# Routing of seven image pairs placed inside the attention-only steps, with the first expert weights loaded early

## The chip, the cores and the metric

The program runs on one core of a Trainium2 chip. A core has a matrix engine (TensorE, PE), three engines for vectors and scalars (VectorE or DVE, ScalarE or ACT, GpSimd or POOL), an engine that mostly issues transfers (SyncE, SP) and 16 DMA engines. Each engine takes its own instructions in program order, and the engines wait for one another through semaphores. SP and ACT issue DMAs on queues of their own; GpSimd issues DMAs through software. The metric is the time of one execution on the device, in microseconds. Before the change three runs took 10483.3 to 10494.0 us, with a median of 10486.95 us.

## What is computed

The input is 16 images of 128 channels and 64 x 64 pixels, which make 16 batches of 4096 tokens. Layer 0 adds a state-space block: a group norm, projections, a short convolution and a scan over time with 16 states for each of 256 channels. Layer 1 adds a causal attention with 8 heads and then a mixture of 64 experts. In the mixture each expert chooses its 8 best tokens of each batch, over the whole of the batch:

```python
t = t + _L1_attn_ref(_ln_t(t), ...)
t = t + _L1_ffn_ref(_ln_t(t), gate_w, gate_b, weight1, weight2)
...
logits = jnp.einsum('bsd,ed->bse', x, gate_w) + gate_b
probs = jax.nn.softmax(logits, axis=1)              # over the tokens
vals, idx = jax.lax.top_k(probs.transpose(0, 2, 1), K)
...
pooled = jnp.einsum('bked,bke->bed', gathered, topv)
h = gelu(pooled @ weight1 + bias1)                  # per expert
out = h @ weight2 + bias2
weighted = jnp.einsum('beo,bke->bkeo', out, topv)
outputs = zeros.at[flat_idx].add(weighted)          # back to the tokens
```

So the routing of a batch needs the logits of all its 4096 tokens, and the experts need the routing of all the batches. "Routing" below is everything from the tokens after attention to the pooled vectors: the layer norm's statistics, the logits, the softmax over tokens, the eight largest, the gate weights (zero outside the chosen tokens) and their product with the normed tokens.

## The kernel before

The work is cut into 128 blocks, 8 of 512 tokens in each batch. The main loop runs over steps `k`. In step `k` the scan of block `k` is made, with the attention of block `m = k - 9` beside it. Each step has 16 rows, one for each state `n`. In a row VectorE makes the product `bx` and two halves of a scan `h`, GpSimd multiplies `h` by the broadcast row `bct` into `da`, and the table `STEP` (line 725) names the other operations of the row: those in its first part come ahead of the scan, those in the second between the scan's halves, those in the third after it. All are issued through `InOrder`, which keeps each engine's instructions in the order of the program.

Names of the table that matter here: `k0` to `k7` are the keys of eight heads, `s0` and `s1` the scores, `mx` and `less` the running maximum (VectorE), `w0` and `w1` the weights of the two halves of a block, `a..` the attention sums, `to0` and `to1` (`take_o`, line 703) the copy of half a block of output, tokens on partitions, into `ot`. In the next step `tu0`, `tu1` (`turn_o`, line 708) turn it to channels on partitions and `fin0`, `fin1` (`finish`, line 715) copy it and store it in `t2_d` from ScalarE's queue. `lnap` makes the normed block `xn`. `spread` loads small pieces of the scores through SP after they were stored in `pd`.

Short tiles (`ot`, `tx`, keys `kt` and others) come from the pool `tmp`, which has six buffers (line 226), taken in turn. The broadcast rows come through SP three rows ahead (`load_bc`, line 369), into five buffers; SP waits for GpSimd to release one. TensorE's results share a pool of three banks (`bank`).

The scans end with step 127. Steps 128 to 137 hold what is left of attention: step 128 finishes the last scanned block, and steps 129 to 136 have one whole attention block each. Step 137 has the second half of the last one.

Then the pools are closed, and the routing runs as a stage of its own (lines 858 to 1048), in 64 iterations. An iteration takes one 512-token block of two batches, a pair. It loads `t2_d` with channels on partitions (SP), turns it on TensorE, takes the statistics on VectorE and makes the normed tokens `xn` on ScalarE, eight activations. The logits come out with tokens on partitions (16 small matmuls), are scaled, and are turned back so that experts lie on partitions. After eight iterations `choose` (line 975) takes the exponential, the eight largest and the gate weights `g`, stored in `g_d`. Twelve iterations behind, `g` is turned and multiplied with the `xn` that were kept.

The experts follow (line 1071), in 16 groups of four. Each group loads 2 MB of weights through SP into four buffers, and its result is stored in `o_d`. The last stage (line 1107) multiplies the experts' results by `g` and adds them to the tokens.

Of the kernel before, what the change touches and what calls it, by code (L numbers as in the profile page):

```python
# [15 lines left out]
P = 128  # L16
# [23 lines left out]
def conv_attn_hybrid(ctx: ExitStack, tc: tile.TileContext, x, w_in, conv_w, conv_b, w_xproj, w_dt, b_dt,  # L40
# [26 lines left out]
    t2_d = dram.tile([NB, C, T], F32, name="t2_d")  # L67
    g_d = dram.tile([NB // 2, P, T], F32, name="g_d")
# [13 lines left out]
    with ExitStack() as st:  # L82
# [3 lines left out]
        yps = st.enter_context(tc.tile_pool(name="yps", bufs=1, space=PSUM))  # L86
        bps = st.enter_context(tc.tile_pool(name="bps", bufs=1, space=PSUM))
# [26 lines left out]
        wv = wp.tile([P, HD, P], F32, name="wv")  # L114

# [101 lines left out]

        xp = st.enter_context(tc.tile_pool(name="xp", bufs=1))
        xsp = st.enter_context(tc.tile_pool(name="xsp", bufs=2))
        xbp = st.enter_context(tc.tile_pool(name="xbp", bufs=2))  # L220
        mp = st.enter_context(tc.tile_pool(name="mp", bufs=2))
        m1 = st.enter_context(tc.tile_pool(name="m1", bufs=1))
        dap = st.enter_context(tc.tile_pool(name="dap", bufs=13))
        hp_ = st.enter_context(tc.tile_pool(name="hp", bufs=2))
        bcp = st.enter_context(tc.tile_pool(name="bcp", bufs=5))
# [481 lines left out]

        def turn_o(m, f):
            s = att[m]
            s["to"] = bank("to_ps")  # L710
            ot = s.pop("ot")
            for q in range(2):
                PE.transpose(s["to"][:, bass.ts(q, P)], ot[:, bass.ts(q, P)], ident)

        def finish(m, f):
# [5 lines left out]

        LAG = NBLK + 1
# [4 lines left out]
            ("k3 k4 skip k5 tu0 fin0", "", ""),  # L727
# [6 lines left out]
            ("ge4 xproj", "tu1 fin1 cen v0 y5", "bcs"),  # L734
# [44 lines left out]

        for k in range(NK + LAG + 1):  # L780
            b, i = divmod(k, NBLK)
            cur = k if k < NK else None
# [37 lines left out]
            for f in range(2):  # L820
                ops[f"tu{f}"] = (mp_, lambda m, f=f: turn_o(m, f))
                ops[f"fin{f}"] = (mp_, lambda m, f=f: finish(m, f))
# [18 lines left out]
            for n in range(N):  # L841
# [13 lines left out]
                do(n, 2)  # L855

# [3 lines left out]
    ff = ctx.enter_context(tc.tile_pool(name="ff", bufs=1))  # L860
    pooled = ff.tile([P, E, 32], F32, name="pooled")
    nc.gpsimd.memset(pooled, 0.0)
    with ExitStack() as st:
        PE, DVE, ACT, POOL, SP = (InOrder(tc, e) for e in (nc.tensor, nc.vector, nc.scalar, nc.gpsimd, nc.sync))
        NG = CB * 2
        LATE = 12
        AHEAD = 5
        xps = st.enter_context(tc.tile_pool(name="rxps", bufs=2, space=PSUM))
        lps = st.enter_context(tc.tile_pool(name="rlps", bufs=1, space=PSUM))
        sps = st.enter_context(tc.tile_pool(name="rsps", bufs=1, space=PSUM))  # L870
        acc = st.enter_context(tc.tile_pool(name="racc", bufs=1, space=PSUM))
        big = st.enter_context(tc.tile_pool(name="big", bufs=2))
        tsp = st.enter_context(tc.tile_pool(name="tsp", bufs=12))
        xnp = st.enter_context(tc.tile_pool(name="xnp", bufs=LATE + 3))
        rp_ = st.enter_context(tc.tile_pool(name="rp", bufs=2))

        def bank():
            return sps.tile([P, CB, P], F32, tag="s", name="s_ps")

        cmat = rp_.tile([P, P], F32, name="cmat2", bufs=1)  # L880
        DVE.tensor_tensor(cmat, ident, mean_w, ALU.subtract)
        gn = rp_.tile([E, C], F32, name="gn", bufs=1)
        SP.dma_start(gn, gate_w)
        gb = rp_.tile([P, 1], F32, name="gb", bufs=1)
        for j in range(2):
            SP.dma_start(gb[j * E : (j + 1) * E, :], gate_b.unsqueeze(1))
        gt_ps = bank()
        PE.transpose(gt_ps[:, 0, :E], gn, ident[:E, :E])
        gt = rp_.tile([P, E], F32, name="gt", bufs=1)
        DVE.tensor_copy(gt, gt_ps[:, 0, :E])  # L890
        gc_ps = bank()
        PE.matmul(gc_ps[:, 0, :E], cmat, gt, start=True, stop=True)
        gtc = rp_.tile([P, E], F32, name="gtc", bufs=1)
        DVE.tensor_copy(gtc, gc_ps[:, 0, :E])
        tc.keep_in_program_order(nc.scalar.preload_act_table_set(EXP_LN))

        NIT = NB // 2 * NBLK
        blk, pair = {}, {}

        def load_tokens(it):  # L900
            p, i = divmod(it, NBLK)
            w = blk[it] = {}
            w["t"] = [tsp.tile([P, L], F32, tag="t", name="t") for _ in range(2)]
            for j in range(2):
                SP.dma_start(w["t"][j], t2_d[2 * p + j, :, bass.ts(i, L)])

        def turn(it):
            w = blk[it]
            w["x"] = xps.tile([P, CB, 2, P], F32, tag="x", name="x_ps")
            for c in range(CB):  # L910
                for j in range(2):
                    PE.transpose(w["x"][:, c, j, :], w["t"][j][:, bass.ts(c, P)], ident)
# [9 lines left out]
        def stats(it):  # L922
# [3 lines left out]
            for g in range(NG):  # L926
                DVE.bn_stats(s6[:, g, :], w["x"][:, g // 2, g % 2, :])
# [220 lines left out]
```

## Time and profile before

| what | value |
|---|---|
| median of three runs | 10486.95 us |
| profiled execution, its own time | 10479.5 us |
| its span, first to last instruction | 10477.5 us |
| TensorE busy | 8614.8 us, 82% |
| VectorE busy | 9138.0 us, 87% |
| ScalarE busy | 7589.4 us, 72% |
| GpSimd busy | 7169.5 us, 68% |
| DMA traffic | 1783.37 MB, mean 170 GB/s |
| mean granted TensorE clock | 0.916 of full speed |

Busy shares are means over stages with different limits. The scans fill most of the span and keep VectorE at 0.9, so a share of the whole says little of the stages after them; those are read from windows of their own. In a group's row the busy time is the union of its instructions' intervals, while the mean is that of one instruction from start to end; where matmuls overlap, the busy time divided by the count is what one more of them costs.

### The profile page before, as it was taken

What the parts mean: (1) busy time and instruction counts of PE and PEld (TensorE: products, weight loads), DVE (VectorE), ACT (ScalarE), POOL (GpSimd) and SP (SyncE); (2) the same over time, 40 slices, a digit from 0 to 9 for tenths busy, and PEclk for the clock granted to TensorE, in tenths of its full rate; (3) what the DMA queues carried; (4) which work ended last, traced back from release to release, by engine and by line L of the source; (5) the groups of instructions that cost most, each with busy time, mean ns of one, the idle gap of its engine ahead of it and who ended that gap; (6) DMA issues with size and microseconds to landing.
All of it is one profiled execution on the core that took longest, in us unless ns stands there. A gap on an engine that the chain in (4) does not pass through costs nothing.

```text
span 10477.5 us, 183327 instructions
## 1 busy us (share of the span) xinstructions
PE 8614.8 (82%) x69084; PEld 5193.8 (50%) x69084; DVE 9138.0 (87%) x9089; ACT 7589.4 (72%) x14186; POOL 7169.5 (68%) x4476
## 2 busy tenths in 40 slices
PE   5578888888888888888888888888888888877775
PEld 3345554555555545554555554555555555544652
DVE  8999999999999999999999999999999999921743
ACT  5568777777777777777777777777787777755740
POOL 7887777777777777777777777777777777710000
PEclk7789999999999999999999999999999999999886
DMA  6676666666676666666666667666666666621358
GB/s 165 171 184 172 178 170 181 164 174 177 166 183 171 181 169 176 173 181 165 172 181 169 181 164 185 168 179 170 178 173 168 177 168 180 163 66 44 115 164 342
DMA packets 978008, 1783.37 MB, mean 170 GB/s; under 512 B 194953, under 2 KB 275489, under 8 KB 967905
## 3 DMA queue, kind: packets, MB, share of 16 engines
q1 hardware_dynamic: 724480, 1381.32, 45.4%
q0 software_dynamic: 82944, 302.03, 14.6%
q10 hardware_dynamic: 169696, 88.30, 3.0%
q8 instruction: 544, 8.91, 0.3%
q14 instruction: 344, 2.81, 0.1%
HBM read 1363.99 MB, written 138.94 MB: 143 GB/s over the span
## 4 chain that ended last, share of the span: by engine, by line
PE 26%; DVE 23%; ACT 20%; DMA 11%; issue 8%; POOL 4%; SPq 1%; ACTq 0%; DVEq 0%; POOLq 0%
DVE h L31 10%; DVE bx L31 8%; ACT da L31 6%; PE k_ps L31 5%; DMA da<-da 5%; PE ao_ps L31 5%; PE v_ps L31 4%; POOL da L31 4%; PE y_ps L31 4%; DMA bct<-bcs 3%; ACT L31 3%; DVE zl L31 2%; PE s_ps L31 1%; ACT xn L31 1%; DMA pd<-parts 1%
## 5 line engine op out<-in xcount | busy, mean ns | idle before, releaser
L31 POOL TENSOR_TENSOR da<-h,bct 128x1024 f32<-128x1024 f32 x2048 | 6334.3, 3098 | 1966.0 <-DVE h L31 766.2
L31 DVE TENSOR_TENSOR_SCAN h<-da,state,bx 128x512 f32<-128x512 f32 x3584 | 4399.7, 1266 | 187.6 <-DVE bx L31 1.9
L31 DVE TENSOR_TENSOR bx<-du,bct 128x1024 f32<-128x1024 f32 x2048 | 2892.8, 1412 | 272.3 <-DMA bct<-bcs 214.0
L31 ACT ACTIVATE da<-delta,a_neg 128x512 f32<-128x512 f32 x4096 | 2676.5, 718 | 73.1 <-DMA da<-da 47.1
L31 PE MATMUL y_ps<-ident,da 128*128 128x128 f32 x12288 | 1795.9, 299 | 632.0 <-POOL da L31 563.3
L31 PEld LDWEIGHTS y_ps<-ident,da 128*128 128x128 f32 x12288 | 1563.1, 155 | 1139.2 <-POOL da L31 624.5
L31 PE MATMUL k_ps<-xn,wk 128*128 128x512 f32 x2048 | 1087.4, 670 | 9.7 <-DVE xn L31 9.7
L31 PE MATMUL v_ps<-wv,xn 128*64 128x512 f32 x4096 | 1031.8, 612 | 75.9 <-ACT v L31 65.0
L31 PE MATMUL xs_ps<-xb,wc 128*128 128x512 f32 x2048 | 974.4, 608 | 1.8 <-issue 1.8
L31 ACT ACTIVATE v<-v_ps 128x512 f32<-128x512 f32 x1024 | 599.9, 596 | 369.7 <-PE v_ps L31 365.4
L31 ACT ACTIVATE kt<-k_ps 128x512 f32<-128x512 f32 x1024 | 609.3, 597 | 328.5 <-PE k_ps L31 317.8
L31 ACT ACT_TABLE_LOAD x633 | 812.1, 1283 | 21.1 <-ACT dbl L31 3.9
L31 PE MATMUL ao_ps<-v,wm 128*64 128x128 f32 x8192 | 608.5, 295 | 219.9 <-ACT wm L31 219.9
L31 PEld LDWEIGHTS ao_ps<-v,wm 128*64 128x64 f32 x8192 | 478.5, 146 | 336.2 <-ACT wm L31 282.7
L31 DVE TENSOR_TENSOR_SCAN h<-da,bx 128x512 f32<-128x512 f32 x512 | 598.1, 1207 | 27.1
L31 PEld LDWEIGHTS k_ps<-xn,wk 128*128 128x128 f32 x2048 | 415.2, 219 | 415.1 <-issue 322.8
L31 POOL COPY state<-h 128x2 f32<-128x2 f32 x1792 | 620.7, 346 | 0.0
L31 PEld LDWEIGHTS xs_ps<-xb,wc 128*128 128x128 f32 x2048 | 364.4, 193 | 470.2 <-issue 375.2
L31 ACT COPY yt<-y_ps 128x512 f32<-128x512 f32 x256 | 137.5, 589 | 624.2 <-PE y_ps L31 624.2
L31 PEld LDWEIGHTS v_ps<-wv,xn 128*64 128x64 f32 x4096 | 224.7, 135 | 674.7 <-ACT v L31 269.9
L31 POOL DMA_DIRECT2D da<-da x512 | 461.7, 902 | 99.3 <-POOL state L31 66.1
L31 PE MATMUL z_ps<-xb,wz 128*128 128x512 f32 x512 | 284.8, 639 | 118.5 <-ACT xc L31 100.3
(208 smaller groups left out, 10480.6 us busy)
## 6 DMA issues: line engine op xcount, KB each, us to landing
bct<-bcs SPq DMA_DIRECT2D x2048, 512.0 KB
da<-da POOLq DMA_DIRECT2D x512, 512.0 KB, 7.5
xs<-t_d SPq DMA_DIRECT2D x240, 256.0 KB
xs<-in_x_dram SPq DMA_DIRECT2D x128, 256.0 KB
t_d<-xt SPq DMA_DIRECT2D x64, 512.0 KB
t_d<-tx ACTq DMA_DIRECT2D x256, 128.0 KB
t<-t_d SPq DMA_DIRECT2D x128, 256.0 KB
tc<-t_d SPq DMA_DIRECT2D x16, 2048.0 KB
```

What stands on the lines that cost most here:

```text
L31: return lambda *args, **kw: self.tc.keep_in_program_order(f(*args, **kw))
```

## The change

Attention's output is stored a second time, with tokens on partitions, in a new array `t2t_d` (`store_tokens`, two SP stores of 128 KB for each block, `st0` and `st1` in the table). This is done in all steps with attention, those beside scans among them.

The scan's pools are put on the other side of the memory, so that they can be closed after step 128. In their place a class `routing` opens pools of its own: 4 of the 8 banks, and buffers for its tiles. From step 129 on, after each row, `route.row` is called; two rows make a slot. A slot treats up to one block of a pair in each of three phases, which follow one another through the steps:

- statistics: GpSimd loads token rows (`xa`), VectorE takes eight `bn_stats`. At the end of a step, `scales` makes the inverse deviations of a pair from these without `bn_aggr`. They are turned and stored in `rs_d`.
- logits: SP loads `t2_d` (`rt`) and the inverse deviations broadcast over the experts (`rb`); two matmuls with 512 columns give the logits with experts on partitions, and VectorE multiplies them into `lg`. The gate matrix is centred once, in the prologue.
- pooling: GpSimd loads the token rows again (`xd`). TensorE turns `g`, VectorE scales it by the inverse deviation, and TensorE multiplies it with the raw tokens. The mean is taken out at the end of a pair (`center_pooled`).

`choose` (row 15), `mark` (row 1) and `keep_chosen` (rows 2 and 3) of a pair come one and two steps later. `g` is no longer divided by the sum of exponentials; that division goes to `center_pooled` and to the last stage. Seven pairs are routed in this way. The last pair's statistics run there too, but for the last block. The rest of it is done after the loop, in `rest`, ahead of which SP issues the loads of the first four groups of expert weights. Weights have five buffers in place of four.

```diff
+        def store_tokens(m, f):
+            b, i = divmod(m, NBLK)
+            at = i * L + f * (L // 2)
+            SP.dma_start(t2t_d[b, at : at + L // 2, :].rearrange("(q p) c -> p q c", p=P),
+                         att[m]["ot"][:, : 2 * P].rearrange("p (q c) -> p q c", c=C))
...
+                self.t = pool("rtt", 4)
+                self.xa = pool("rxa", 3)
+                self.xd = pool("rxd", 2)
+                self.rb = pool("rrb", 2)
...
+            def load_stats(self, it):
+                p, i = divmod(it, NBLK)
+                x = self.w["a", it] = self.xa.tile([P, CB, 2, P], F32, tag="xa", name="xa")
+                for j in range(2):
+                    POOL.dma_start(x[:, :, j, :], t2t_d[2 * p + j, bass.ts(i, L), :].rearrange("(c p) d -> p c d", p=P))
...
+            def logits(self, it):
+                l = self.w["l", it] = self.lps.tile([P, L], F32, tag="l", name="l_ps")
+                t = self.w.pop(("t", it))
+                for j in range(2):
+                    PE.matmul(l[j * E : (j + 1) * E, :], gtc, t[j], start=True, stop=True)
...
+            def choose(self, p):
...
+                w["top"], w["den"] = top, self.sm.tile([P, 1], F32, tag="den", name="den")
+                ACT.activation(w["g"], w["lg"], AF.Exp, bias=neg, accum_out=w["den"])
+
+            def mark(self, p):
+                w = self.pair[p]
+                DVE.match_replace(out=w["lg"], in_to_replace=w.pop("top"), in_values=w["lg"], imm_value=NEG)
...
+                if half == 0:
+                    for it in at(D0 + 1, EARLY):
+                        self.pool_chosen(it)
+                    for it in at(B0, EARLY):
+                        self.logits(it)
+                    for it in at(D0, EARLY):
+                        self.turn_chosen(it)
...
+                    return
+                for it in at(D0, EARLY):
+                    self.scale_chosen(it)
+                for it in at(B0, EARLY):
+                    self.keep_logits(it)
+                for it in at(1, 8, 2) + [x for x in at(6 - 8, EARLY) if x >= 8]:
+                    self.stats(it)
...
+                for it in at(0, 8, 2) + [x for x in at(5 - 8, EARLY) if x >= 8]:
+                    self.load_stats(it)
...
+                for it in at(B0 - 1, EARLY):
+                    self.load_scales(it)
+                for it in at(B0 - 2, EARLY):
+                    self.load_logits(it)
+                for it in at(D0 - 1, EARLY):
+                    self.load_chosen(it)
+
+            def row(self, r):
+                step, n = divmod(r, N)
+                self.slot(r // 2, n % 2)
+                if step < NPR - 1:
+                    if n == 11:
+                        self.scales(step)
...
+                if n == 15 and 1 <= step <= NPR - 1:
+                    self.choose(step - 1)
+                if 2 <= step <= NPR:
+                    if n == 1:
+                        self.mark(step - 2)
+                    if n in (2, 3):
+                        self.keep_chosen(step - 2, n - 2)
...
+        B0, D0 = 8, 18
...
-            ("k3 k4 skip k5 tu0 fin0", "", ""),
+            ("k3 k4 skip k5 st0 tu0 fin0", "", ""),
...
-            ("ge4 xproj", "tu1 fin1 cen v0 y5", "bcs"),
+            ("ge4 xproj", "st1 tu1 fin1 cen v0 y5", "bcs"),
...
+                if route is not None:
+                    route.row((k - NK - 1) * N + n)
...
+    WAHEAD = 4
+    for e0 in range(0, WAHEAD * EG, EG):
+        load_weights(e0)
+    route.rest()
...
             nc.sync.dma_start(on, o_d[2 * pr : 2 * pr + 2].rearrange("b e o -> (b e) o"))
+            nc.vector.tensor_scalar(on, on, rden[:, pr : pr + 1], None, ALU.mult)
```

## The prediction

> **What bounds the kernel now.** I read the page first, for the slices of the span, then the busy times of four stretches, then the groups of instructions inside the routing stage, the waits of the attention-only steps, and last the order of time in one steady step and among the experts.
>
> The page's slices, each a fortieth of the span (262 us), in tenths:
>
> ```profile
> DVE  8999999999999999999999999999999999921743
> ...
> POOL 7887777777777777777777777777777777710000
> ...
> DMA  6676666666676666666666667666666666621358
> ```
>
> For 35 slices VectorE is at 0.9: the scans. Then VectorE and GpSimd fall to almost nothing, though the kernel runs for 1,250 us more. The windows split this tail (columns: us, then busy us and count of PE, PEld, DVE, ACT, POOL, then clock, DMA share, GB/s):
>
> ```profile
> 9436.00:9477.00 41.00, 33.02 (x344) 17.68 (x338) 2.11 (x7) 24.59 (x53) 0.00 (x0) 0.96 0.09 24
> ...
> 9750.00:9850.00 100.00, 79.47 (x704) 70.37 (x706) 79.05 (x295) 71.45 (x181) 0.00 (x0) 0.90 0.36 117
> ...
> 10175.00:10246.00 71.00, 52.78 (x500) 20.04 (x492) 8.16 (x17) 4.78 (x8) 0.00 (x0) 0.62 0.72 223
> 10246.00:10360.00 114.00, 67.75 (x124) 29.45 (x124) 39.34 (x61) 0.00 (x0) 0.00 (x0) 0.62 0.88 361
> ```
>
> The first is one attention-only step (period 41.9 us): TensorE and ScalarE hand work to each other, VectorE works 2.1 us, GpSimd not at all, DMA 0.09. The second is routing, where TensorE, VectorE and ScalarE are all busy; the third the experts, the fourth the last sum, which the transfers bound. The last scan starts at 9229.3, the last attention store is issued at 9641, the first weights' load at 10106.7 and the last sum's first load about 10246; I put the borders at 9231 (attention only), 9643 (routing), 10107 (experts) and 10246, so they last 412, 464, 139 and 231 us.
>
> Groups in the routing stage (busy us, mean ns, idle before):
>
> ```profile
> L31 ACT ACTIVATE xn<-x_ps,nm,rs 128x128 f32<-128x128 f32 x512 | 185.5, 474 | 0.0
> ...
> L31 DVE BATCH_NORM_STATS2 s<-x_ps 128x6 f32<-128x128 f32 x512 | 107.3, 285 | 10.8 <-PE x_ps L31 10.6
> ...
> L31 PE MATMUL pl<-xn,gT 128*64 128x128 f32 x1024 | 76.6, 297 | 0.0
> ...
> L31 DVE TENSOR_TENSOR ls<-l_ps,rs 128x512 f32<-128x512 f32 x64 | 43.9, 686 | 0.3 <-PE l_ps L31 0.3
> L31 PE MATMUL s_ps<-ident,g 128*128 128x128 f32 x256 | 43.0, 295 | 5.7 <-DVE g L31 3.2 <-ACT gT L31 1.7 <-ACT lg L31 0.8
> ...
> L31 DVE MAX8 top<-lg 128x8 f32<-128x1024 f32 x32 | 38.5, 1202 | 1.9 <-ACT lg L31 1.7 <-issue 0.3
> L31 DVE SCALAR_TENSOR_TENSOR g<-g,sden,rep 128x2048 f32<-128x2048 f32 x16 | 37.3, 2334 | 0.0
> ...
> L31 DVE MATCH_REPLACE8 rep<-top,lg 128x4096 f32<-128x4096 f32 x8 | 35.3, 4409 | 0.0
> ...
> L31 ACT ACTIVATE g<-lg,neg 128x4096 f32<-128x4096 f32 x8 | 30.1, 3757 | 0.0
> ```
>
> Back-to-back matmuls overlap, so I price TensorE by a group's busy time over its count, not by the mean. In the attention steps' groups the keys give the price of a 512-column matmul:
>
> ```profile
> L31 PE MATMUL k_ps<-xn,wk 128*128 128x512 f32 x128 | 58.9, 603 | 0.0
> ```
>
> that is 0.46 us. And in time order, in a steady step of the main loop, ScalarE's attention output, the key five places on, and GpSimd's product that frees the SP queue's next buffer:
>
> ```profile
> 5040.88 0.36 ACT L31 COPY ot<-ao_ps 128x256 f32<-128x256 f32 x1
> ...
> 5056.95 0.58 ACT L31 ACTIVATE kt<-k_ps 128x512 f32<-128x512 f32 x1
> ```
> ```profile
> 5037.54 2.36 POOL L31 TENSOR_TENSOR da<-h,bct 128x1024 f32<-128x1024 f32 x1 [0.30 <-DVE h L31]
> ```
>
> **The Trainium skill.** "DMA: Bandwidth & Descriptors", section "Anatomy of one DMA — SWDGE (gpsimd) path", gives a fixed cost of about 2 us per DMA from GpSimd and calls descriptor generation "small, variable". The trace has 902 ns on GpSimd per da<-da DMA and 7.5 us to its landing, under the main loop's traffic. The same page, section "Queues, rings and completion order", says that an engine consumes a queue's descriptors in ring order and takes turns between queues; so the early weights delay what SP issues after them, not GpSimd's loads. "Specifications" there asks for at least 512 B per piece; the token rows are just that. Half of the weight bytes before are also 512 B rows, and that stage reached 328 GB/s in one 8 us window.
>
> **The change, part by part.**
>
> *Main loop.* The engines' order is unchanged. Added are two SP stores of 128 KB per step, 119 steps with attention before the scans end. A store holds the buffer of ot until it has landed, and `tmp` has six: the sixth key, kt at 5056.95, takes that buffer. SP reaches st0 when GpSimd's product above is done (5039.9), waits for ot (5041.2), and should land by about 5045: 12 us to spare. Behind SP's wait stand the B/C loads, but the next one needs a GpSimd product that ends at 5048. st1 waits for ot at 5009.8, 1.5 us before its successor's buffer is free. As engine time, 256 KB at 310 GB/s is 0.8 us a step, 100 us in all if nothing covered it; VectorE's waits for bct come behind the small spread loads, 11 us after st1. I take 5 us; bounds 0 and 100. The gate's preparation moves to the prologue, about 1 us, left out.
>
> *Removed.* The 464 us stage. Gone outright are the transposes of x, 512 xn activations (185 us of ScalarE), the turning of logits and its copies. Removing the aggregation and not_equal spares VectorE too.
>
> *Moved.* One block per two rows, eight per step, in nine steps. Per block TensorE: pooling 76.6/64 = 1.20, turn of weights 43.0/64 = 0.67, two logits matmuls 0.92: 2.8 us, 22.3 per full step. VectorE: eight stats 2.28, scaling 0.69, logits 0.69, max 0.60: 4.25 us a block, 34 a step, with match_replace 4.4, two products 4.7, the last pair's block 2.3 and small ones 1.5 it is 47, and 49 with attention's 2.1. ScalarE: 24.6 + 4.0 (the exponential) + 0.6 = 29. Transfers: xa, xd and rt 4.2 MB each, rb and g_d 2.1 each, attention 1.2: 18 MB, at 310 GB/s 58 us. GpSimd: 32 DMAs. Its price is not shown for 512 pieces: at da's 0.9 us it is 29 us, in proportion to pieces (128 there) 3.6 us, 115 a step. I take 1.2 us, 38 a step, since the skill calls generation small; both ends go to the range.
>
> So TensorE needs 33 + 22.3 = 55 us a full step, transfers 58, VectorE 49. They are in-order and coupled. Of the 8.9 us that TensorE waits today I let blocks cover 5 to 6 (its waits for wm stand right behind a block) and keep 3. New: at row 15 `choose` puts 4 us on ScalarE, and behind it the table load and all keys; its bias waits for VectorE to finish block 15 (5 us). TensorE has three banks of keys and one block (5.5 us) before it stops; it loses about 5.4. VectorE's mark and products stand ahead of `mx` in rows 1 to 3, and xd is loaded only 1.5 blocks ahead: 4 us together. Sum 33 + 22.3 + 3 + 5.4 + 4 = 68 us. Steps that are not full: k=129 has no TensorE blocks (44), k=130 logits only (50), k=131 (62), then four of 68, k=136 without xa loads (65), k=137 has half an attention step, 25 us, and eight blocks (45). From 9273 that is 538: 9811.
>
> *Last pair, `rest`.* Drain of five blocks 12; SP's loads behind 8.4 MB of weights (27 us, begun in the middle of the last step) 5; eight logits, each load 0.75 MB reissued two ahead, 2.5 each: 20; choose, mark (which must wait for the exponential, as it writes lg in place) and two products 13.5; eight poolings over two xd buffers, each pair about 8.6 us (two DMAs of 1.2, landing 5, pooling 1.2) from the third on: 29; centre and turn 2. Sum 82: 9893.
>
> *Experts.* Five groups of weights can be there. Without missing weights a group takes TensorE and its hand-overs 7.2 to 7.4 us before (hs at 10164.09, 10171.53); 16 make 117, with the end 121, against 139. The other 11 groups are 23 MB, 75 us, hidden. *Last sum*: eight small scalings more; 231.
>
> Sum: 9893 + 121 + 231 + 5 = 10250 as span. The profiled execution took 10479.5, 2.0 more than its span, and 7.5 less than the median of the runs shown; I forecast 10255 us.
>
> **The rivals.**
>
> *GpSimd's issuing and the transfers bound the steps.* At 3 us per DMA a block takes 12 us, a full step 96. Four steps lose 112, the two beside them about 30, the last pooling 10: 10405 us. For it: four DMAs of 512 pieces per block, and DMA already at 58 us. Against it: GpSimd is otherwise empty.
>
> *The waits are all covered.* Blocks fill TensorE's waits and a full step takes 58, the transfers' time: 45 to 60 us less, 10200 us. For it: ScalarE at 0.6. Against it: `choose` ahead of the keys.
>
> *Slower: the token stores hold up the main loop.* Place: SP's queue at st0 and st1, whose late landing stops ScalarE at the sixth key and the B/C loads behind. It decides from 1.9 us per step (227 us of gain over 119 steps); at 3 us it costs 357 and gives 10612 us. For it: 119 repetitions, and VectorE already waits 214 us for bct. Against it: the 12 us to spare, and bct loads three rows ahead.
>
> That the blocks don't run beside attention at all, with routing at its old pace, would give about 10480; I see nothing that would order them so.
>
> **How the numbers follow.** Forecast 0.60; GpSimd or transfers 0.17; waits covered 0.12; slower 0.09; no change 0.02. The range, 10180 to 10390, holds the forecast, the covered case and half of the GpSimd case. Faster by over 0.2% (about what a measurement of this kernel can tell): 0.89; within 0.02; slower 0.09.
>
> **What would show it.** The scans still end near 9231, and kt has no wait on t2t_d; attention-only steps of 60 to 75 us from k=132 on, with keys waiting behind g; GpSimd's DMAs near 1.2 us; experts' first hps near 9895 and groups 7.3 us apart. Scans that end 50 us later, or GpSimd busy throughout those steps, would prove it wrong.

## The result, and the profile after

The changed kernel took 10331.53 us (median of four runs, 10323.3 to 10338.42), the kernel before 10488.61 us in the runs beside it (10483.3 to 10494.0): a ratio of 0.985 with a 95% interval from 0.9833 to 0.9867. The profiled execution took 10338.42 us, the slowest of its four, with a span of 10336.7 us.

The page's slices, for the same rows as before, in tenths of each fortieth of the span:

```profile
DVE  8999999999999999999999999999999999984533
...
POOL 7887777777777777777777777777777777773310
...
DMA  6676766667676666666676667666676766657878
```

The 37th and 38th slices (9303 to 9820 us) are the attention-only steps: VectorE is at 0.4 and 0.5 there, GpSimd at 0.3, DMA at 0.7 and 0.8. Before, four fifths of the 37th slice (9430 to 9641 us) were attention-only, and the slice has 0.1, 0 and 0.1. In the windows (us, then busy us and count of PE, PEld, DVE, ACT, POOL, then clock, DMA share, GB/s) the first is a full attention-only step, the second what comes after attention, the third the experts, the fourth the first half of the last sum:

```profile
9536.78:9608.13 71.35, 56.72 (x550) 32.17 (x548) 42.26 (x117) 29.09 (x58) 25.22 (x35) 0.88 0.85 249
9884.00:10000.00 116.00, 52.98 (x326) 28.45 (x322) 36.45 (x60) 5.69 (x5) 21.07 (x28) 0.69 0.79 234
10000.00:10105.00 105.00, 89.65 (x960) 33.33 (x960) 15.65 (x32) 10.84 (x17) 0.00 (x0) 0.92 0.74 226
10105.00:10220.00 115.00, 66.28 (x136) 29.29 (x136) 42.21 (x70) 0.00 (x0) 0.00 (x0) 0.69 0.92 377
```

A full step has TensorE at 57 of 71 us, VectorE at 42 and the DMA engines at 0.85, where the step before the change had 33 of 41, 2 and 0.09. Cut at the starts of the last scan, of attention's last copy `tx`, of the first `hps` (the experts' first matmul) and of the experts' last copy `os`, the profiled executions split like this (us; "forecast" is put together from the prediction's terms, with step 137's 45 us cut into its 25 us of attention and 20 us of routing, and the 5 us of the main loop put where they belong):

| stage | before | forecast | after | after less forecast |
|---|---|---|---|---|
| start to the last scan | 9229.3 | 9234.3 | 9283.5 | +49.2 |
| to attention's last copy | 411.7 | 561.7 | 600.0 | +38.3 |
| to the first `hps` | 470.7 | 102 | 116.6 | +14.6 |
| experts | 133.3 | 121 | 104.7 | -16.3 |
| rest of the span | 232.5 | 231 | 231.9 | +0.9 |
| span | 10477.5 | 10250 | 10336.7 | +86.7 |

Attention and routing together took 882 us before and take 717 after, a gain of 166; the experts gain 29; the main loop gives 54 back. These come to 141 us, and the medians to 157: the profiled execution of the kernel before (10479.5 us) was faster than each of its four timed runs, and that of the changed kernel was the slowest of its four. So some 16 us of the last column can be scatter between executions.

TensorE's price of a block came out as forecast. These are groups of the four full steps, 32 blocks (busy us, mean ns, idle before):

```profile
L31 POOL DMA_DIRECT2D xd<-t2t_d x64 | 47.6, 748 | 123.7 <-PE pl_ps L31 123.4 <-issue 0.2
...
L31 PE MATMUL pl_ps<-xd,gT 128*64 128x128 f32 x512 | 35.5, 282 | 0.0
L31 PE MATMUL l_ps<-rt,gtc 128*64 128x512 f32 x128 | 34.0, 597 | 2.1 <-DMA rt<-t_d 2.1
...
L31 PE MATMUL gp_ps<-ident,g 128*128 128x128 f32 x128 | 21.0, 287 | 0.0
```

A block costs TensorE 35.5/32 for pooling, 34.0/32 for the logits and 21.0/32 for the turn of the weights: 2.83 us, where 2.8 was forecast. GpSimd's DMA takes 748 ns where 1.2 us was taken. What was larger than forecast is the main loop, the full step and the stretch after attention, and the experiments are about these three.

### The profile page after: what moved, and what is told of

It is laid out like the page before. It is cut to its first block, busy times and chain, and to the rows that moved or that the text cites. A ratio compares the mean times of both kernels' runs of the same rounds, so it can differ in the third digit from the quotient of the medians.

```text
span 10336.7 us, 179924 instructions
## 1 busy us (share of the span) xinstructions
PE 8433.0 (82%) x67556; PEld 4977.0 (48%) x67556; DVE 9091.4 (88%) x8648; ACT 7303.3 (71%) x13426; POOL 7335.0 (71%) x4732
## 3 DMA queue, kind: packets, MB, share of 16 engines
q0 software_dynamic: 103424, 369.15, 17.0%
## 5 line engine op out<-in xcount | busy, mean ns | idle before, releaser
L31 PE MATMUL k_ps<-xn,wk 128*128 128x512 f32 x2048 | 1109.7, 681 | 63.6 <-ACT kt L31 32.5
L31 PE MATMUL v_ps<-wv,xn 128*64 128x512 f32 x4096 | 1030.1, 612 | 74.8 <-ACT v L31 68.9
L31 DVE TENSOR_TENSOR_SCAN h<-da,bx 128x512 f32<-128x512 f32 x512 | 597.9, 1207 | 28.5 <-ACT kt L31 0.5
L31 POOL DMA_DIRECT2D da<-da x512 | 459.2, 897 | 99.5 <-POOL state L31 65.7
```

The source lines that it names most:

```text
L31: return lambda *args, **kw: self.tc.keep_in_program_order(f(*args, **kw))
```

## The experiments

Ratios are to runs of the kernel before on the same chip.

### The main loop

After the change VectorE's product `bx` waits longer for the broadcast rows; the page's group, before and then after (busy, mean ns, idle before and what ended most of it):

```profile
L31 DVE TENSOR_TENSOR bx<-du,bct 128x1024 f32<-128x1024 f32 x2048 | 2892.8, 1412 | 272.3 <-DMA bct<-bcs 214.0
```
```profile
L31 DVE TENSOR_TENSOR bx<-du,bct 128x1024 f32<-128x1024 f32 x2048 | 2864.6, 1399 | 352.2 <-DMA bct<-bcs 294.2
```

The wait ended by `bct` has grown by 80 us. By the prediction, those rows come behind the small loads of `spread` on SP. The timeline of SP in one step of the changed kernel (start, us, operation):

```profile
5028.00 0.36 SPq L31 DMA_DIRECT2D t2t_d<-ot  x1
5029.92 0.36 SPq L31 DMA_DIRECT2D bct<-bcs  x1
5039.41 1.23 SPq L31 DMA_DIRECT2D lh<-pd  x4
5040.68 0.29 SPq L31 DMA_DIRECT2D rh<-pd  x1
5041.01 1.25 SPq L31 DMA_DIRECT2D lh<-pd  x4
5042.31 0.28 SPq L31 DMA_DIRECT2D rh<-pd  x1
5042.69 5.85 SPq L31 DMA_DIRECT2D bct<-bcs  x5
```

and VectorE beside it (idle before, in brackets):

```profile
5043.22 2.45 DVE L31 TENSOR_TENSOR_SCAN h<-da,state,bx 128x512 f32<-128x512 f32 x2
5047.72 1.52 DVE L31 TENSOR_TENSOR bx<-du,bct 128x1024 f32<-128x1024 f32 x1 [2.06 <-DMA bct<-bcs]
```

SP issues nothing from 5030.28 to 5039.41: the next in its order is the first `lh` load, which needs the scores that ScalarE sent to `pd` at 5034.78. Then ten small loads take 3.2 us to issue, the next `bct` leaves at 5042.69, and VectorE waits 2.06 us for it. This happens in nearly every step: of the waits for `bct`, 246 of 294 us fall in this place, row 13 (189 of 214 before). Two experiments try the stores, and the small loads.

**e1, the stores alone.** The kernel before, with the token stores and nothing else of the change.

```diff
-            ("k3 k4 skip k5 tu0 fin0", "", ""),
+            ("k3 k4 skip k5 st0 tu0 fin0", "", ""),
...
-            ("ge4 xproj", "tu1 fin1 cen v0 y5", "bcs"),
+            ("ge4 xproj", "st1 tu1 fin1 cen v0 y5", "bcs"),
```

> The kernel before with the two token stores per step added and nothing else. In the changed kernel the last scan starts at 9283.5 us, before at 9229.3. Theory: the stores alone make these 54 us, as traffic and as waits on SP's queue ahead of the B/C loads. Then the last scan starts at 9275 to 9290, VectorE's waits for bct rise from 214 to about 290 us, and the whole is 50 to 60 us (0.5%) slower than before. Rival: the moved pools and the prologue make them. Then the last scan stays within 10 us of 9229 and the time within 0.1% of before.

Measured: 10497.73 us, ratio 1.0014 (1.0005 to 1.0023), so 14 us (5 to 24). Its profiled execution was the slowest of its eleven:

```profile
L31 DVE TENSOR_TENSOR bx<-du,bct 128x1024 f32<-128x1024 f32 x2048 | 2860.1, 1397 | 343.3 <-DMA bct<-bcs 285.2
```

The waits for `bct` are 285.2 us in it, 245 of them in row 13, so the stores alone put these waits nearly where the change has them. The last scan starts 39.5 us later than before. So the stores do cost something, by way of the `bct` waits. Whether they make the whole of the 49 us that the forecast missed is not settled: the profiles of three kernels with the change's main loop (after, e2, e4) have the last scan at 9283.5, 9273.6 and 9266.6, that is 37 to 54 us later than before, and 14 us by the timed runs is less than that. The longer prologue is not the rest: the first scan starts at 51.7 us after the change and at 50.6 before. The moved pools were not run alone.

**e3, fewer small transfers.** The changed kernel, with `pd` laid out so that SP needs four loads for the scores instead of ten (ScalarE needs four stores instead of one). The loads of `rh`, left out here, change to match.

```diff
-            s["pd"] = bcd.tile([3, 2, P, 64], BF16, tag="pd", name="pd")
-            ACT.dma_start(s["pd"].rearrange("t w p s -> p (t w) s"), s.pop("parts").rearrange("p t w s -> p (t w) s"))
+            s["pd"] = bcd.tile([HD // 2, 3, 2, 32, 64], BF16, tag="pd", name="pd")
+            parts = s.pop("parts").rearrange("p t w s -> p (t w) s")
+            for x in range(HD // 2):
+                ACT.dma_start(s["pd"][x].rearrange("t w r s -> r (t w) s"), parts[32 * x : 32 * x + 32])
...
-                for x in range(HD // 2):
-                    row, of = 64 + 12 * u + 3 * x, 32 * x + 16 * u
-                    SP.dma_start(lh[row : row + 3, :, u, :], pd[:, 0, of : of + NC8, :])
+                row = 64 + 12 * u
+                SP.dma_start(lh[row : row + 12, :, u, :],
+                             pd[:, :, 0, 16 * u : 16 * u + NC8, :].rearrange("x t r s -> (x t) r s"))
...
```

> The changed kernel with the score pieces laid out in memory so that SP's ten small loads per step become four (ScalarE's one store becomes four). Theory: it is the path store of pd, small loads, then B/C row 13 and w0 that costs, in the main loop (VectorE waits 2.1 us a step for bct at row 13) and in the attention-only steps (TensorE waits 7 to 14 us for rh at w0). SP's issuing falls from 3.2 us to 1.3 us, so VectorE's waits for bct fall from 294 us to about 100, the last scan starts 120 to 200 us sooner, and the full attention-only steps fall from 71 to about 68 us. Rival: the landing of pd, not SP's issuing, sets these waits, or ScalarE's three further stores cost as much. Then the last scan moves by less than 40 us and the full steps stay at 70 us or more.

Measured: 10161.04 us, ratio 0.9692 (0.9677 to 0.9706): 170 us better than the changed kernel. SP's timeline in the same step:

```profile
5022.32 0.36 SPq L31 DMA_DIRECT2D bct<-bcs  x1
5031.69 0.32 SPq L31 DMA_DIRECT2D lh<-pd  x1
5032.06 0.29 SPq L31 DMA_DIRECT2D rh<-pd  x1
5032.39 0.29 SPq L31 DMA_DIRECT2D lh<-pd  x1
5032.73 0.29 SPq L31 DMA_DIRECT2D rh<-pd  x1
5033.06 7.81 SPq L31 DMA_DIRECT2D bct<-bcs  x5
```

The four loads take 1.4 us, and the wait for `pd` is no shorter (9.0 us from the end of one issue to the next). The 1.9 us saved on the queue are about what the waiting product lacked (2.06 us): the waits for `bct` fall to 70.6 us, and the last scan starts at 9113.0. The other half of what this run was to tell, the full step, did not move: 70.2 us in the mean of four. TensorE's wait for `rh` was gone (at most 0.7 us), but the time was not; here ScalarE's copies `tx` wait 28.5 us in the four steps behind the stores to `pd`.

**e5, the same edit without the change.** The kernel before with e3's edit only.

> The kernel before with only the merged score transfers of e3 (four loads on SP in place of ten, four stores on ScalarE in place of one; no routing moved). If VectorE's waits for bct stand behind the small loads of the spread on SP, whatever else is changed, they fall here from 214 us to about 70 as in e3 and the last scan ends near 9100: time about 10350, ratio 0.987, and e3's gain over after (170 us) splits into about 130 that was there before the change and about 40 that the change had added. If the long bct waits of the main loop come from the token stores, the merge brings nothing here: 10484.

Measured: 10354.29 us, ratio 0.9866 (0.9848 to 0.9883). The group of `bx` on its page:

```profile
L31 DVE TENSOR_TENSOR bx<-du,bct 128x1024 f32<-128x1024 f32 x2048 | 2922.1, 1427 | 112.7 <-DMA bct<-bcs 52.4
```

The last scan starts at 9093.7, 136 us sooner than before; e3's starts 170 us sooner than the changed kernel's. So most of what e3 wins was there to be had before the change. With this edit in both, the change itself gives 0.9692/0.9866 = 0.982. What it costs the main loop is smaller there: the eight kernels with the change and this edit have the last scan between 9094.4 and 9137.6, 9115 in the mean, 21 us after e5's. That is one profile of e5 against a spread of 43 us among the eight, so the size is rough.

### The full step

In the four full steps of the changed kernel the engines wait most for these (us in total, times, longest):

```profile
POOL xd L31 <- PE pl_ps L31: 123.4, 28, 13.7
...
DVE lg L31 <- DMA rb<-rs_d: 58.2, 10, 10.2
...
ACT g L31 <- DVE neg L31: 28.2, 4, 7.9
...
PE w_ps L31 <- DMA rh<-pd: 26.3, 4, 7.6
...
PE k_ps L31 <- ACT kt L31: 21.7, 4, 5.4
```

GpSimd's wait for the last pooling only says that it is ahead. Candidates are the late `rb` (VectorE), the late `rh` (TensorE), `choose` ahead of the keys, and the transfers behind them all. Against the late `rh` speaks e3, and e7 below more: there the waits for `rh` and for the stores to `pd` are both short (1.3 and 5.7 us in four steps), and the step is still 69.7 us.

**e4, a short exponential.** The changed kernel with the exponential of `choose` over 512 of 4096 columns, and weights 1 at the chosen tokens.

```diff
-                ACT.activation(w["g"], w["lg"], AF.Exp, bias=neg, accum_out=w["den"])
+                ACT.activation(w["g"][:, :L], w["lg"][:, :L], AF.Exp, bias=neg, accum_out=w["den"])
...
-                DVE.scalar_tensor_tensor(g, lg, NEG, g, ALU.is_equal, ALU.mult)
+                DVE.scalar_tensor_tensor(g, lg, NEG, bc(ones[:, 0:1], [P, T // 2]), ALU.is_equal, ALU.mult)
```

> The changed kernel with the exponential of choose over 512 of 4096 columns (7/8 of the exponentials are left out, and the gate weights are 1 at the chosen tokens). Theory of the prediction: the exponential stands ahead of the keys at row 15 and costs TensorE about 5 us in each of six steps; then 3.2 us a step go, the full steps fall from 71 to about 68 us, and the first hps matmul comes 20 to 25 us sooner, 3 of them from the last pair's own exponential. Rival: the step's end is set by the path of pd and rh, and the keys' wait only moves there; then the full steps stay at 70 us or more.

Measured: 10307.05 us in one run, full steps of 71.2 us in the mean, against 72.2. TensorE's wait for the keys fell from 21.7 to 15.7 us in four steps, but the step hardly did. Something else came late instead, among it the landing of the token stores, for which ScalarE's keys now wait:

```profile
ACT kt L31 <- DMA t2t_d<-ot: 17.8, 4, 5.3
```

**e6, token rows once per pair.** e3, with `xa` and `xd` loaded for the first block of a pair only; the computing stays, on the first block's rows. The edit of `xd` (that of `xa` is alike):

```diff
+                if i and it < NIT - NBLK:
+                    self.w["d", it] = self.one_d
+                    return
                 x = self.w["d", it] = self.xd.tile([P, CB, 2, P], F32, tag="xd", name="xd")
+                if it < NIT - NBLK:
+                    self.one_d = x
```

> e3 with the token rows for the statistics and for the pooling loaded once per pair instead of once per block (7/8 of xa and xd left out for the seven pairs, all computing kept; the values are those of the pair's first block). It takes some 7 of 18 MB and 28 of 32 GpSimd DMAs from a full step. If the transfers set the full step of 70 us, it falls to 60 or less (11 MB at 255 GB/s are 43 us, then TensorE's 55 us with its waits bounds), and the time to about 10161 - 50 = 10110. If the hand-overs between TensorE and ScalarE set it, it stays at 67 to 71 and the time at 10150.

Measured: 10111.39 us in one run. Two full steps of e3, then of e6 (columns as above):

```profile
9362.94:9431.48 68.54, 56.06 (x549) 30.52 (x548) 42.15 (x117) 28.90 (x57) 25.01 (x34) 0.93 0.91 271
9431.48:9501.31 69.83, 56.93 (x548) 30.86 (x547) 42.15 (x117) 28.37 (x58) 24.71 (x35) 0.90 0.91 265
```
```profile
9355.28:9416.76 61.48, 52.81 (x550) 29.98 (x548) 42.23 (x117) 28.96 (x58) 4.44 (x6) 0.94 0.64 184
9416.76:9478.23 61.47, 52.96 (x550) 29.93 (x548) 42.26 (x118) 28.97 (x58) 4.45 (x6) 0.94 0.62 184
```

The step falls from 70.2 to 61.5 us, the same in all four steps, while TensorE's, VectorE's and ScalarE's instructions are the same ones. DMA goes from 0.90 to 0.63 in the mean of four. So these loads make some 9 us of the full step. GpSimd's issuing of them goes too, but GpSimd is busy for only 25 of e3's 70 us. The waits for `rb` are gone, and the keys are the longest wait left on TensorE:

```profile
PE k_ps L31 <- ACT kt L31: 21.7, 4, 5.4
...
DVE lg L31 <- DMA rb<-rs_d: 2.0, 3, 0.8
```

Less than half of the 8.7 us is waiting, though: TensorE's idle time falls by 3.9 us a step and its busy time by 4.8, from 57.6 to 52.7 us for the same matmuls. The trace's clock records show what goes with it. In these steps TensorE's granted clock is either full or half, and in e6 it is at half speed once in each step, for 6.8 us that begin about 2 us into the wait for the keys. One such stretch of e6, which begins inside the wait that ends at 9400.5:

```profile
9397.00:9403.80 6.80, 3.29 (x4) 1.51 (x5) 6.18 (x10) 5.01 (x7) 0.00 (x0) 0.50 0.31 96
```

In e3 the half-speed stretches come to 12 us a step; some of them follow waits of 1.6 to 2.6 us for loads or for ScalarE. In the changed kernel they come to 16 us, and three of the four that follow the waits for `rh` are 10.2 us long. So a wait on TensorE seems to cost more than its own length. That the waits bring the slow stretches is read from their order in time and was not tried by itself.

**e11, both.** e6 with e4's edit.

> e6 with e4's short exponential too (gate weights 1 at the chosen tokens, 7/8 of the exponentials left out), to see what choose costs a step once the transfers don't bind. As the prediction has it, the exponential ahead of the keys costs TensorE 5.4 us a step, of which 3.3 go here (3.76 us become 0.47): full step 61.5 - 3 = 58 and the time about 10095. If something else ends last, the step stays 61.5 and the time 10111.

Measured: 10072.68 us in one run; two full steps:

```profile
9343.22:9400.06 56.84, 51.15 (x550) 29.32 (x548) 42.05 (x117) 26.11 (x58) 4.44 (x6) 1.00 0.66 198
9400.06:9458.98 58.92, 53.13 (x550) 29.81 (x548) 42.15 (x117) 25.89 (x58) 4.46 (x6) 0.97 0.67 192
```

The mean of four is 58.1 us, 3.4 below e6, where 3.3 was expected. TensorE's wait for the keys falls from 21.7 to 9.8 us in four steps. So the exponential of `choose` does stand ahead of the keys and costs about its own length; in e4 that didn't show, since other things came late there. The trace of the changed kernel shows the place, first ScalarE and then TensorE:

```profile
9660.67 3.71 ACT L31 ACTIVATE g<-lg,neg 128x4096 f32<-128x4096 f32 x1 [7.88 <-DVE neg L31]
9664.28 0.19 ACT L31 ACTIVATION_READ_ACCUMULATOR g<-lg,neg 128x1 f32 x1
9664.49 1.28 ACT L31 ACT_TABLE_LOAD   x1
9665.78 1.57 ACT L31 ACTIVATE kt<-k_ps 128x512 f32<-128x512 f32 x3
```
```profile
9666.43 5.43 PE L31 MATMUL k_ps<-xn,wk 128*128 128x512 f32 x6 [5.43 <-ACT kt L31]
```

**e10, `rb` two rows sooner.** e3 with three buffers of `rb`, issued one slot earlier but for the first block of a pair (and `xa` in two buffers, for room).

```diff
-                for it in at(B0 - 1, EARLY):
+                for it in [x for x in at(B0 - 1, EARLY) if x % NBLK == 0] + [x for x in at(B0 - 2, EARLY) if x % NBLK]:
```

> e3 with rb in three buffers and issued two rows sooner (but for the first block of a pair); xa has two buffers in place of three for the room. The same bytes in each step. If it is the late rb on SP's queue (VectorE's 45 us in four full steps, which holds the logits' bank and what VectorE has behind) that makes a full step 70, the wait goes to under 10 us and the step to 61 to 65: time 10120 to 10140. If the DMA engines' capacity bounds the step, the wait turns up at another transfer and the step stays 68 to 71: 10161.

Measured: 10135.8 us, ratio 0.9672 (0.9659 to 0.9685). VectorE's wait for `rb` in four full steps went from 45.2 to 1.2 us, and the step from 70.2 to 68.9 us. A late `rb` was a sign of busy DMA engines, more than a cause: without that wait their share rose from 0.90 to 0.93 in the mean, and the step hardly moved. The whole is 25 us better than e3, as if `rb` did cost something; but of the 19 us between the two profiles 11 lie in the main loop, which this edit doesn't touch. A cost of `xa`'s lost buffer, which may hide a part of the gain, was not tried.

**e7 and e9, longer pieces.** e7 is e3 with four tokens to a partition in memory, so that a piece there is 2 KB; `rb` and `g` are read with a stride. e9 also lays the tile out so that its side of the piece is 2 KB. The lines are from e9:

```diff
-                x = self.w["a", it] = self.xa.tile([P, CB, 2, P], F32, tag="xa", name="xa")
+                x = self.w["a", it] = self.xa.tile([P, 2, CB, P], F32, tag="xa", name="xa")
...
-                    POOL.dma_start(x[:, :, j, :], t2t_d[2 * p + j, bass.ts(i, L), :].rearrange("(c p) d -> p c d", p=P))
+                    POOL.dma_start(x[:, j], t2t_d[2 * p + j, bass.ts(i, L), :].rearrange("(p c) d -> p c d", c=CB))
...
-                    PE.transpose(gp[:, c, :], self.pair[p]["g"][:, i * L + c * P : i * L + (c + 1) * P], ident)
+                    PE.transpose(gp[:, c, :], self.pair[p]["g"][:, i * L + c : (i + 1) * L : CB], ident)
```

> e3 with the token rows loaded four tokens to a partition, so in pieces of 2 KB instead of 512 B (128 in place of 512 for each DMA; the same bytes); VectorE takes the inverse deviations and TensorE the gate weights with a stride of 4 tokens. If the DMA engines are slowed by short pieces, the full step falls from 70 to about 60 to 63 and the time to about 10120. If the bytes set it or the hand-overs do, it stays at 70 and 10161. GpSimd's 747 ns per DMA fall towards da's 900 or below only if the pieces count; if they stay, issue has a fixed price.

> e7 with the tiles xa and xd laid out as image, block of 128, channel, so that the pieces are 2 KB on both sides (in e7 they were 2 KB only in memory, 512 B in the tile, and its count of packets was e3's). GpSimd's queue should count some 400 packets less per load. If the number of pieces loads the DMA engines, DMA share falls from 0.90 in a full step, the step from 70 to 62 to 66, and the time to 10120 to 10145. If bytes alone do, it is 70 and 10161. GpSimd's price per DMA falls below 747 ns if it goes by pieces.

Measured: e7 10169.6 us, ratio 0.9695 (0.9681 to 0.971), step 69.7: no difference from e3. e9 10120.48 us, ratio 0.9657 (0.9644 to 0.967), step 65.7. In both, VectorE works 3 us more in a step than in e3 (45 against 42): the strided product with `rb` takes 1043 ns instead of 685. Of the 43 us between the profiles of e9 and e3, 23 lie between the last scan and attention's last copy; 19 lie in the main loop, which is the same in both. Two full steps of e9:

```profile
9344.20:9408.14 63.94, 55.09 (x551) 31.26 (x549) 45.20 (x117) 29.02 (x58) 18.07 (x35) 0.95 0.89 277
9408.14:9476.96 68.82, 56.02 (x549) 31.21 (x550) 45.05 (x118) 28.89 (x58) 18.03 (x35) 0.95 0.88 284
```

GpSimd's group for `xd` over the whole span, e3 and then e9:

```profile
L31 POOL DMA_DIRECT2D xd<-t2t_d x128 | 95.4, 750 | 272.8 <-PE pl_ps L31 270.1 <-PE gp_ps L31 2.0 <-issue 0.6
```
```profile
L31 POOL DMA_DIRECT2D xd<-t2t_d x128 | 68.4, 539 | 297.4 <-PE pl_ps L31 276.3 <-PE gp_ps L31 14.0 <-issue 7.1
```

With the same bytes, and the DMA engines at 0.90 of the time in both, the four full steps of e9 move 283 GB/s where e3's move 263, and GpSimd issues an `xd` DMA in 539 ns instead of 750. Which of these two shortens the step was not separated. A piece has to be long on both sides: e7's was 512 B in the tile, and changed neither number (264 GB/s, 750 ns). The profile's count of packets can't tell this. The expectation had it falling, but GpSimd's queue has 103,424 in e3, e7 and e9 alike; e6, with 196 DMAs less, has 15,680 less, 80 for each 256 KB; so these two cuts count alike.

**e12, e9 and e10 together.**

> e9 with e10's sooner rb (and two buffers of xa). With long pieces VectorE still waits 23 us for rb in four full steps. If a late rb costs now that the transfers have some room, the full step goes from 65.7 to 62 to 64 and the time to about 10105. If, as e10's step of 68.9 against 70.2 says, the DMA engines' load sets the step, it changes by under 1.5 us a step: 10110 to 10125, no difference from e9 that can be told.

Measured: 10131.98 us, ratio 0.9657 (0.9644 to 0.967), step 64.6: as in e10, about 1 us a step, and no difference from e9 in the whole. e9 and e12 are the best of the kernels that leave nothing out, at 0.9657 of the kernel before, where the changed kernel has 0.985.

### After the loop

**e2 and e8, weights later.** The first four groups of expert weights are issued behind the last pair's loads for the logits; e2 is the changed kernel with this, e8 is e3 with it.

```diff
-    for e0 in range(0, WAHEAD * EG, EG):
-        load_weights(e0)
-    route.rest()
+    route.rest(lambda: [load_weights(e0) for e0 in range(0, WAHEAD * EG, EG)])
```

> The changed kernel with the first four groups of weights issued behind the last pair's logits loads instead of ahead of them. Theory: the weights hold SP's queue for 34 us (9884 to 9918), and the last pair's logits start only at 9932. Then the logits start 20 to 27 us sooner, the first hps matmul comes at about 9975 in place of 10000, the experts still take about 105 us, since the weights have 30 us beside choose, mark and pooling, and the whole is about 20 to 25 us (0.2%) faster than the changed kernel. Rival: the weights are then missing at the experts' start. Then the experts take 120 us or more and the sum stays as it is.

> e3 with e2's late weights as well. If e2's 20 us come from the last pair's logits loads no longer standing behind 8 MB of weights, they are here too: 10161 - 15 to 20 = 10143, with the last logits about 15 us sooner after the end of attention. If e2's gain was only the main loop's scatter (its last scan ended 10 us sooner than in the profile of after), it is 10161.

Measured: e2 10311.52 us, ratio 0.9836 (0.9819 to 0.9852); e8 10165.88 us, ratio 0.969 (0.9675 to 0.9705), no difference from e3. In both the last logits come sooner after attention, as expected (60.3 us in e2 and 60.2 in e8, against 74.9 after and 74.5 in e3), but from attention's last copy to the first `hps` e2 needs 116.5 us, and after 116.6. It is lost again in the last pair's eight poolings, here after and then e2:

```profile
9975.70:9998.10 22.40, 15.86 (x152) 11.55 (x152) 4.70 (x7) 0.00 (x0) 8.93 (x12) 0.93 0.62 197
```
```profile
9941.20:9976.20 35.00, 22.96 (x152) 16.92 (x152) 4.72 (x8) 0.00 (x0) 8.93 (x12) 0.70 0.87 274
```

With the weights in flight beside them, TensorE waits longer for GpSimd's `xd` loads, and its clock is lower. In e8 the poolings take 34 us as well, and its experts take 111 us where e3's take 107. e2's profile is 10 us shorter in the main loop and 12 in the steps, which this edit doesn't touch, so its 20 us are not shown to be its doing.

## Why the prediction was right, and where it was off

The mechanism held: seven pairs' routing fits into steps in which TensorE and ScalarE waited for each other, at the price of longer steps; the experts go faster; the time fell by 157 us by the medians, where 232 was forecast (10255 us), inside the range.

It is inside in part by luck. Main loop, attention and the last pair took 102 us more than forecast together, the experts 16 less for a reason that was not foreseen, and the range is wide since it was made to hold half of the GpSimd case, which did not come. Of the signs that the prediction named, the steps of 60 to 75 us and the keys behind `g` came. The others went against it: the scans end 54 us later in the profile, which it had said would prove it wrong; the first `hps` is at 10000 and not near 9895; the groups of experts are 6.5 us apart (104.7/16), not 7.3; GpSimd's DMA costs 0.75 us, not 1.2. The step from a span of 10250 to 10255 us is also not the sum of its two terms, 2.0 and 7.5; nothing rests on that.

By its steps:

- *Main loop, 5 us with bounds 0 and 100.* Measured 54 in the profile, the largest miss. The first part of the reasoning was right: the sixth key waits for a token store once in the whole run, 2.7 us. The second part was written down and priced too low: "VectorE's waits for bct come behind the small spread loads, 11 us after st1". There the queue had no slack, as e3 and e5 show by what 1.9 us on it are worth. By e1 the stores make 14 us of it in the timed runs. That they lengthen this wait is seen in e1's profile; how they do it, as traffic or by holding SP, was not separated, and the rest of the miss is open.
- *The forecast's rival, stores that hold up the main loop.* Its place was right, its size was not: about 0.1 us a step by e1, 0.45 by the profile, against the 1.9 from which it decides.
- *The full step, 68 us.* Measured 72.2 in the mean of four. Its terms: TensorE's work 55 forecast, 56.9 measured, at a mean clock of 0.89. VectorE's 49 forecast, 42 measured: the statistics were priced by their mean of 285 ns, where busy time over count gives 0.21 us before and 0.20 after. `choose` 5.4 forecast; TensorE's wait is 5.4 us at 9666.43 and 21.7 us in four steps, and e11 shows that the step loses 3.4 us with seven eighths of the exponential, but only where the transfers leave room. Transfers 58 us at 310 GB/s and so hidden: this is the term that failed. The steps moved 257 GB/s in the mean with the DMA engines at 0.88 (a longer step by itself lowers this rate), and although that left them some idle time, the transfers were not hidden: e6 gives the price of 7 of the 18 MB in e3's step, 8.7 us. The 3 us kept of the old waits and the 4 us for `mark`, the products and late `xd` loads were not measured one by one; with `choose` they came to 12.4 us of waiting, where TensorE is idle for 15.2. So the sum came near though its terms leave out a cost that the prediction had listed under a rival: that is luck too.
- *GpSimd, 1.2 us per DMA with bounds 0.9 and 3.6.* Measured 748 ns, below the lower bound. The rival "GpSimd's issuing and the transfers bound the steps" was half right: the transfers cost 8.7 us (e6), while GpSimd was busy for 25 of the step's 72 us. What its issuing costs by itself was not separated.
- *The rival in which all waits are covered, a step of 58 us.* Not reached by the changed kernel. e11's step is 58.1 us, with 7 MB less and a short exponential, but not for the prediction's reason, that 58 us of transfers bound it: its DMA engines are at 0.66.
- *The last pair, 102 us after attention.* Measured 116.6. The last logits matmul starts 74.9 us after attention's last copy, where 20 + 12 + 5 + 20 = 57 were forecast; SP's weights took 34 us to issue (9884.32 to 9918.38), and the last pair's loads stood behind them; this is the term with 5 us. Moving them won that back and lost it later (e2, e8). The prediction had the early weights delay what SP issues after them, "not GpSimd's loads". The runs differ: in e2 and e8 the poolings, fed by GpSimd, took 35 and 34 us with weights in flight, against 22 after. With the weights ahead they were cheaper than the forecast 29.
- *Experts, 121 us.* Measured 104.7: TensorE's busy time is 90 of 105 us at a granted clock of 0.92, where the clock before was 0.62. The prediction took the hand-overs of before at their old duration. Why the clock is higher, and what the fifth buffer does in it, was not tried.
- The Trainium skill ("DMA: Bandwidth & Descriptors", "Specifications") asks for at least 512 B a transfer for full rate, and the prediction rested on the token rows being "just that". The runs differ: in the full steps, 2 KB pieces on both sides gave 283 GB/s where 512 B gave 263 (e9 and e3). That page's section "Anatomy of one DMA — SWDGE (gpsimd) path" calls the making of descriptors "small, variable"; by e9, 0.2 of an `xd` load's 0.75 us depend on the pieces.

## What to carry to other kernels

When work is moved into a stage that has idle engines, sum its bytes at the rate that the same mix of pieces really reaches, and don't count transfers as hidden when they keep the DMA engines busy for nearly all of the stage (0.88 here). In such a stage, taking away one engine's wait may move the time little (e10), and a wait for a small load can be a sign of busy DMA engines. Where an in-order queue already waits in every step, look at what it issues between the end of that wait and what the busiest engine needs next; fewer transfers there were worth 1.3% (e5), nearly as much as the whole change (1.5%). And when one suspected cost seems to be worth nothing, try it again with the other taken away before you call it free.

## What the hardware showed that was not expected

- SP spends about 0.31 us on each small load (four in 1.23 us), so ten of them hold back the queue by 3.2 us.
- TensorE's clock in the full steps is full or half (1.0 or 0.5 in the records). In e6 each step has one half-speed stretch of 6.8 us, and each begins about 2 us into the wait of 5.4 us for the keys; in e11, where that wait is 2.4 us, three of four steps have one of 3.4 us and one step has none.
- A load of `xd` by GpSimd, 256 KB, costs it 750 ns with 512 B pieces (e3) and 539 ns with 2 KB pieces on both sides (e9); pieces that are long in memory only cost 750 ns (e7). Accumulating loads of 512 KB (`da`) cost 897 ns.
- SP's issue of the early weights took 1.7 us per DMA (34.06 us for 20), where before the change four of the first ones took 0.7 us each (2.81 us from 10106.68).
